# Two layer norms behind the last MLP of a four-layer transformer: later turns, the first applied by ScalarE

## The chip, the cores and the metric

The kernel runs on one core of a Trainium2 chip. The metric is the device time of one execution in microseconds, lower is better. The numbers shown are the median of several executions, and one execution that the hardware profiler recorded. The engines are called PE (TensorE, matrix products), DVE (VectorE), ACT (ScalarE), POOL (GpSimd) and SP (SyncE, which issues the DMAs); PEld is TensorE's loading of weights.

## The reference

Eight blocks in a row, each added to the residual stream `x` with a norm in front and one behind. The input has 16 sequences of 256 tokens with 128 features, all float32. The part that matters here is the end of the third block and the beginning of the fourth:

```python
x = x + layernorm(L1_attn(layernorm(x)))     # block 3: a transformer of its own
x = x + layernorm(L1_ffn(layernorm(x)))      # block 4: soft mixture of 64 experts

def L1_attn(z):                              # four layers
    for i in range(4):
        z = z + attention(layer_norm(z, g1, b1)) # 4 local heads, 4 linear heads
        h = layer_norm(z, g2, b2)
        z = z + (gelu(h @ W1[i] + b1[i]) @ W2[i] + b2[i])
    return z

def L1_ffn(m):
    logits = einsum('bmd,dnp->bmnp', m, phi)
    dispatch = softmax(logits, axis=0)       # over the batch
    combine = softmax(logits over n*p)
    slots = einsum('bmd,bmnp->bnpd', m, dispatch)
    return einsum('bnpd,bmnp->bmd', einsum('bnpd,nde->bnpe', slots, W) + b, combine)
```

Two norms without gain or bias stand between the inner transformer's last MLP and the mixture of experts: the norm of the inner result `z`, which is added to `x`, and the norm of the new `x`, which is the mixture's input `m`. A norm is (v − mean) / sqrt(var + 1e-5) over the 128 features of a token.

## The kernel before

The tokens are cut into eight groups of 512 (two sequences each). A group's data is a tile of 128 partitions by 4 token tiles by 128 features, and stays in SBUF: `x[g]` is the outer residual stream, `z[g]` the inner transformer's. The stage is `stage_l1_attn`. It makes two generators for each of 4 layers x 8 groups: `l1_mix` (attention) and `ffn` (the MLP and, in the last layer, what follows it). Each generator yields between its steps. `k.turns` goes through turns; in each turn every generator that has started is moved on by one step (up to three where it is behind its place), the latest one first. Groups start 8 turns apart, and a group's `ffn` starts 17 turns after the group's nominal start. The engines then run their instructions in the order in which they were so written (`tc.manual_schedule`); `idle(n)` is n turns in which a generator writes nothing. So a number of idle turns decides behind which instructions of the other groups a step stands in every engine's queue.

The names that matter for the steps:

- `k.stats(v)`: four `bn_stats` (L255) and four `bn_aggr` (L257) on VectorE give mean and variance (`ln_st`, `ln_mv`), and GpSimd makes the reciprocal root `ln_rs` in two instructions on 128x4 elements, a multiply-add (L244) and a power (L245).
- `k.stats_nb(v)`: the same, and two more GpSimd instructions on 128x4 (L274, L275) for `ln_nb`, minus mean times root.
- `k.normed`: applies a norm with four VectorE instructions of 128x128 (L264). `k.normed_act` applies it with four ScalarE activations of 128x128, scale `ln_rs` and bias `ln_nb` (L283).
- `k.residual(x, y, wait)`: stats of y, `wait` turns, `k.normed` into `ln_y`, and a GpSimd add of 128x512 into x (L303).
- `then(g, wait)` is `fill` of `soft_inputs`: a DMA copies `x[g]` to DRAM (`xs`, 256 KB, SP's queue), then `stats_nb(x[g])`, `wait` idle turns, and `normed_act` into `mxn[g]`, the mixture's input.
- `l1_ffn`: norm of z into `xn` (stats, a turn, L264 on VectorE), three turns, four transposes on TensorE (L325), ScalarE's `xT` (L811), GpSimd's add of the bias row to z (L818, 128x512), the two products with `mlp_h` on ScalarE between (L824), and VectorE's `z` from `ps_o` (L834).
- `l1_mix`: norm and transposes likewise; GpSimd's add of a bias row (L848); `qT`, `kT`; in two halves VectorE's `qm` and `q` (L874, L875) and ScalarE's `kr`, `ke`, `l_val`, `l_lin` (L876 to L879); in two batches the `b_negmask` products and scores on TensorE and VectorE's maxima `l_max` (L899, four of 128x384) with a 128x4 minimum behind (L900); transposes of the maxima (L913); VectorE's `l_ctx` (L936) and GpSimd's (L937); in two batches the exponentials `e` on ScalarE (L949) and two causal masks on GpSimd (L952); products into `ps_o`, ScalarE's `oT` (L969), VectorE's `cat` (L982, L993), ScalarE's `catT` (L999), and VectorE's `z` (L1002).

In this stage PSUM's eight banks are a ring of seven for all tiles but the outputs, and one bank, `ps_o`, which the attention's and the MLP's outputs share. Groups 6 and 7 (`k.over`) take no part in the edited lines: their norms are done inside the next stage.

In the last layer the eight groups pass one after another, one every 22 to 25 us. While a group's MLP and norms run, the next group's MLP and the attention of the ones after it fill the engines; behind group 5's norms no attention is left.

The functions that the diff touches, as in the kernel before:

Of the kernel before, what the change touches and what calls it, by code (L numbers as in the profile page):

```python
# [25 lines left out]
ALU = mybir.AluOpType  # L26
# [3 lines left out]
NB, SEQ, P, D = 16, 256, 128, 128  # L30
NG, NT, GT = 8, 4, 512
# [154 lines left out]
def idle(n):  # L186

    for _ in range(n):
        yield


def bc(ap, axis, n):

    ap = ap.unsqueeze(axis)
    shape = list(ap.shape)
    shape[axis] = n
    return ap.to_broadcast(shape)
# [554 lines left out]
def rest_of_l0(k, x, z, y):  # L752

    yield from k.residual(x, y, 3)
    yield
    nb, rs = k.stats_nb(x)
    yield from idle(3)
    k.normed_act(z, x, nb, rs)


def stage_l1_attn(k, x, ws, rows, z, then, xn, y7, xT0):


    nc = k.nc

    k.l1_val = [k.t([P, NT, 4, 32], f"l1_val{i}", 1) for i in range(3)]
    k.l1_lin = [k.t([P, NT, 65], f"l1_lin{i}", 1) for i in range(3)]
    k.l1_ctx = [k.t([P, 4, 68], f"l1_ctx{i}", 1) for i in range(2)]  # L770
    k.l1_max = [k.t([P, 2, 3, 4, 32], f"l1_max{i}", 1) for i in range(2)]
    for a in k.l1_val + k.l1_lin:
        nc.vector.memset(a, 1.0)
    for a in k.l1_max + k.l1_ctx:
        nc.gpsimd.memset(a, 0.0)
    for a in k.l1_ctx:
        nc.gpsimd.tensor_copy(a[:, :, 64:68], bc(k.c["head16"], 1, 4))
    k.cb = {n: k.t([P, P], "b_" + n, 1, dt=BF16) for n in ("ident", "negmask")}
    for n, a in k.cb.items():
        nc.vector.tensor_copy(a, k.c[n])  # L780

    def ffn(i, g):
        late = i == 3 and g in k.over
        yield from l1_ffn(k, z[g], ws[i], rows[f"b2{i}"], xn[g] if late else z[g])
        if i == 3 and not late:
            yield from idle(2)
            yield from k.residual(x[g], z[g], 2)
            yield
            yield from then(g, 2)

    at = [0, 5, 11, 16, 22] + [32 + 8 * n for n in range(4 * NG - 5)]
    items = []
    for n, start in enumerate(at):
        i, g = divmod(n, NG)
        items.append((start - (0 if n == 0 else 4), l1_mix(k, z[g], ws[i], rows[f"bo{i}"], n, xT0 if n == 0 else None)))
        items.append((start + 17, ffn(i, g)))
    items = sorted(items, key=lambda item: -item[0])
    with k.tc.manual_schedule():  # L800
        k.turns(items + [(0, rest_of_l0(k, x[NG - 1], z[NG - 1], y7))])
# [13 lines left out]
def l1_ffn(k, z, w, b2, out):  # L815

    hT = yield from l1_norm_T(k, z, w["ln2_g"], w["ln2_b"], 1, 3)
    k.nc.gpsimd.tensor_tensor(z, z, bc(b2, 1, NT), ALU.add)  # L818
    yield
    h = k.t([P, 4, GT], "mlp_h", 2)  # L820
    for f in range(4):
        ps = k.ps("s")
        k.mm(ps, w["w1"][:, f * P : (f + 1) * P], hT)
        k.nc.scalar.activation(h[:, f, :], ps, AF.Gelu, bias=w["b1"][:, f : f + 1])  # L824
        if f % 2:
            yield
    ps = k.ps("o").rearrange("p (t d) -> p t d", t=NT)
    w2 = w["w2"].rearrange("p (c n) -> p c n", c=4)
    for t in range(NT):
        for f in range(4):  # L830
            k.mm(ps[:, t, :], h[:, f, t * P : (t + 1) * P], w2[:, f, :], f == 0, f == 3)
        if t in (0, 2):
            yield
    k.nc.vector.tensor_tensor(out, ps, z, ALU.add)  # L834
# [1252 lines left out]
```

## Time and profile before

| quantity | value |
|---|---|
| time, median of 3 executions | 2942.89 us (2938.27 to 2943.25) |
| profiled execution, its own time | 2940.6 us |
| its span | 2938.8 us |
| granted TensorE clock, mean over the span | 0.973 |
| TensorE busy | 2729.7 us, 93% |
| VectorE busy | 1953.3 us, 66% |
| ScalarE busy | 1717.5 us, 58% |
| GpSimd busy | 1017.2 us, 35% |
| instructions | 59589 |
| edited part within the span | about 787 to 930 us |

The span is the time from the first to the last recorded instruction of the profiled execution; what lies around it makes 1.8 us. Busy times are sums over the engine's instructions. In the lines of the profile, a row of a timeline begins with the start and the duration in microseconds, then engine, source line, operation, output and inputs with their shapes, how many instructions were joined (x4), and in brackets the idle time of the engine ahead of it and what ended that. In the table of windows each row has the stretch, its length, the busy time of the engines with the number of instructions, the granted TensorE clock, the DMA share and GB/s.

### The profile page before, as it was taken

How to read it: one execution, taken by the hardware profiler on the slowest of the kernel's cores; microseconds unless marked ns; L12 is line 12 of the kernel's file. 1: busy time of each engine (PE TensorE's matmuls, PEld its weight loads, DVE VectorE, ACT ScalarE, POOL GpSimd, SP SyncE). 2: the span in 40 equal slices, each digit the busy share in tenths (PEclk: the TensorE clock that was granted, in tenths of full speed). 3: DMA queues.
4: the chain of work that ended last, by engine and by line, in shares of the span. 5: the costliest groups of instructions: out<-in, count | busy, mean ns of one | idle time of the engine just before them, and what ended most of it. 6: DMA issues, size and time to landing. Idle time of an engine off the chain costs nothing.

```text
span 2938.8 us, 59589 instructions
## 1 busy us (share of the span) xinstructions
PE 2729.7 (93%) x23673; PEld 1845.0 (63%) x23674; DVE 1953.3 (66%) x5309; ACT 1717.5 (58%) x3568; POOL 1017.2 (35%) x1406
## 2 busy tenths in 40 slices
PE   8889999999998799999978998899999799989998
PEld 4556667766666588888853443566666444436897
DVE  5665666666675989999866765666574677736542
ACT  6756566666665567777735665444444277756443
POOL 3543333333345100000044555422231466545332
PEclk9999999999999899999988999899999899999999
DMA  4000000000000000000020000000000000010000
GB/s 117 12 1 1 2 1 2 2 2 2 5 12 24 1 16 9 8 9 8 9 71 5 1 1 1 1 1 1 1 1 1 2 1 1 1 33 27 2 16 16
DMA packets 29150, 31.30 MB, mean 11 GB/s; under 512 B 7292, under 2 KB 20156, under 8 KB 28732
## 3 DMA queue, kind: packets, MB, share of 16 engines
q1 hardware_dynamic: 28872, 27.49, 3.1%
q8 instruction: 187, 3.06, 0.4%
q14 instruction: 91, 0.75, 0.1%
HBM read 23.29 MB, written 4.19 MB: 9 GB/s over the span
## 4 chain that ended last, share of the span: by engine, by line
PE 69%; ACT 12%; DVE 11%; POOL 5%; issue 2%; DMA 0%; POOLq 0%; SPq 0%; ACTq 0%; DVEq 0%
PE ps_s L336 44%; PE ps_o L336 10%; PE ps_mm L336 6%; PE ps_s L325 3%; ACT e L949 2%; ACT at_e L491 1%; POOL ln_rs L245 1%; ACT lg L1215 1%; DVE xn L264 1%; PE ps_xin L336 1%; ACT meT L1222 1%; POOL e L952 1%; PE ps_sum L336 1%; ACT L949 1%; ACT mdisp L1122 1%
## 5 line engine op out<-in xcount | busy, mean ns | idle before, releaser
L459 DVE TENSOR_REDUCE at_nm<-ps_s 128x2 f32<-128x512 f32 (+1 forms) x384 | 238.1, 682 | 119.6 <-PE ps_s L336 119.6
L491 ACT ACTIVATE at_e<-ps_s 128x512 f32<-128x512 f32 x384 | 198.2, 604 | 97.0 <-PE ps_s L336 94.8
L1504 DVE TENSOR_TENSOR scan<-ps_s,lm 128x384 f32<-128x384 f32 x256 | 124.7, 549 | 142.4 <-PE ps_s L336 142.1
L497 POOL TENSOR_SCALAR_AFFINE_SELECT at_e<-at_e 128x1024 f32<-128x1024 f32 (+1 forms) x96 | 135.1, 1407 | 209.0 <-ACT at_e L491 208.7
L245 POOL TENSOR_TENSOR ln_rs<-ln_rs,mhalf 128x4 f32<-128x4 f32 x192 | 196.1, 1021 | 15.8
L1031 POOL TENSOR_TENSOR ln_rs<-ln_mv,mendt 128x4 f32<-128x4 f32 x6 | 1.2, 200 | 521.0 <-DVE ln_mv L1029 521.0
L244 POOL TENSOR_SCALAR ln_rs<-ln_mv 128x4 f32<-128x4 f32 x184 | 39.6, 215 | 371.2 <-DVE ln_mv L257 352.8
L336 PE MATMUL ps_o<-my,meT 128*128 128x129 f32 x1024 | 142.5, 286 | 22.2 <-ACT mgot L1234 18.4
L336 PE MATMUL ps_s<-l1f_phi,mxT 128*128 128x256 f32 x512 | 141.6, 401 | 21.6 <-DVE mpart L1096 15.9
L899 DVE TENSOR_REDUCE l_max<-ps_s 128x3 f32<-128x384 f32 x256 | 124.8, 551 | 51.4 <-PE ps_s L336 49.1
L952 POOL TENSOR_SCALAR_AFFINE_SELECT e<-e 128x512 f32<-128x512 f32 x128 | 78.9, 637 | 217.2 <-ACT e L949 217.2
L336 PEld LDWEIGHTS ps_o<-my,meT 128*128 128x128 f32 x1024 | 126.3, 193 | 40.5 <-ACT mgot L1234 24.1
L336 PE MATMUL ps_s<-qm,kT 32*128 32x512 f32 x768 | 144.0, 652 | 8.0 <-DVE at_nm L459 7.8
L336 PE MATMUL ps_s<-km,qT 32*128 32x512 f32 x768 | 138.2, 667 | 11.3 <-DVE qT L1648 3.7
L336 PEld LDWEIGHTS ps_o<-l_w,mlp_h 128*128 128x128 f32 x1024 | 126.0, 192 | 19.1 <-issue 12.8
L336 PE MATMUL ps_o<-at_e,at_vm 128*32 128x128 f32 (+1 forms) x2048 | 123.2, 338 | 15.3 <-ACT at_oT L521 15.3
L336 PE MATMUL ps_o<-l_w,mlp_h 128*128 128x128 f32 x1024 | 130.1, 276 | 4.0 <-ACT oT L969 3.9
L336 PE MATMUL ps_s<-b_negmask,b_ident 128*128 128x256 bf16 (+1 forms) x640 | 123.6, 303 | 8.1 <-DVE b_negmask L780 1.4
L1481 ACT COPY BT<-ps_s 128x512 f32<-128x512 f32 x64 | 37.5, 587 | 158.1 <-PE ps_s L336 158.1
L336 PE MATMUL ps_mm<-mdisp,mxn 128*128 128x128 f32 x1024 | 125.3, 279 | 5.0 <-DVE mdisp L1134 4.9
L336 PEld LDWEIGHTS ps_mm<-mdisp,mxn 128*128 128x128 f32 x1024 | 121.8, 195 | 7.9 <-DVE mdisp L1134 6.6
L336 PE MATMUL ps_s<-xT,l_w 128*128 128x512 f32 x256 | 124.4, 607 | 1.3 <-ACT xT L811 1.3
(469 smaller groups left out, 7192.5 us busy)
## 6 DMA issues: line engine op xcount, KB each, us to landing
mw<-in_l1fw SPq DMA_DIRECT2D x16, 256.0 KB, 2.6
moe_w<-in_moe SPq DMA_DIRECT2D x16, 256.0 KB, 5.3
l_w<-in_l SPq DMA_DIRECT2D x10, 256.0 KB, 3.3
x<-in_x SPq DMA_DIRECT2D x8, 256.0 KB, 5.1
xs<-x SPq DMA_DIRECT2D x8, 256.0 KB, 2.1
out<-x SPq DMA_DIRECT2D x8, 256.0 KB, 2.3
slT<-xs SPq DMA_DIRECT2D x6, 256.0 KB, 2.8
l1f_phi<-in_l1f SPq DMA_DIRECT2D x1, 1024.0 KB, 5.0
```

The costliest lines, as they stand in the source:

```text
L244: g.tensor_scalar(out, in_, scale, eps, ALU.mult, ALU.add)
L245: g.tensor_tensor(out, out, self.mhalf[:, :n], ALU.pow)
L325: self.nc.tensor.transpose(out[:n, k * P : (k + 1) * P], src[:, k, cols], self.c["ident"])
L336: self.nc.tensor.matmul(out, lhsT=lhsT, rhs=rhs, start=start, stop=stop, skip_group_check=True)
L459: v_.tensor_reduce(nm[:, t, r, vs], s, AX.X, ALU.max, negate=True)
L491: nc.scalar.activation(e[:, r], s, AF.Exp)
L497: nc.gpsimd.affine_select(at, at, [[0, 4], [0, n], [1, P]], ALU.is_ge, 0.0, base=0, channel_multiplier=-1)
L899: v.tensor_reduce(mx[:, b, :, h, 16], s, AX.X, ALU.max, negate=True)
L949: nc.scalar.activation(e[:, h].rearrange("p j n -> p (j n)"), s[:, : 3 * P], AF.Exp)
L952: nc.gpsimd.affine_select(e[:, :, j, :], e[:, :, j, :], [[0, 4], [1, P]], ALU.is_ge, 0.0, base=0, channel_multiplier=-1)
L1481: nc.scalar.copy(s, ps)
L1504: v.tensor_tensor(m, s[:, : SEQ + P], lm[:, SCAN_HEADS[4 * (t // 2) + 2 * i + hh], :], ALU.mult)
```

## The change

In the last layer, for groups 0 to 5, `ffn` waits six turns instead of two behind the MLP before it takes the statistics of z; it takes them with `stats_nb`, so GpSimd also makes `ln_nb`; three turns later ScalarE, not VectorE, applies the norm (`normed_act` into `ln_y`); GpSimd adds it to x as before; after three turns, not one, `then` copies x to DRAM and takes its statistics, and after three more turns, not two, ScalarE writes `mxn`.

```diff
--- before.py
+++ after.py
@@ -783,10 +783,14 @@
         late = i == 3 and g in k.over
         yield from l1_ffn(k, z[g], ws[i], rows[f"b2{i}"], xn[g] if late else z[g])
         if i == 3 and not late:
-            yield from idle(2)
-            yield from k.residual(x[g], z[g], 2)
-            yield
-            yield from then(g, 2)
+            yield from idle(6)
+            nb, rs = k.stats_nb(z[g])
+            yield from idle(3)
+            y = k.t([P, NT, D], "ln_y", 2)
+            k.normed_act(y, z[g], nb, rs)
+            nc.gpsimd.tensor_tensor(x[g], x[g], y, ALU.add)
+            yield from idle(3)
+            yield from then(g, 3)
```

The written order of TensorE's and of SP's instructions is the same in both kernels. VectorE has 24 instructions fewer, ScalarE 24 more and GpSimd 12 more. Lines of the new code behind the edit stand four lines lower than those of the kernel before; the GpSimd add of x is L791 in the changed kernel.

## The prediction

> **What bounds the kernel now.** I read the page first: busy shares, then the chain of work that ended last.
>
> ```profile
> PE 2729.7 (93%) x23673; PEld 1845.0 (63%) x23674; DVE 1953.3 (66%) x5309; ACT 1717.5 (58%) x3568; POOL 1017.2 (35%) x1406
> PE 69%; ACT 12%; DVE 11%; POOL 5%; issue 2%; DMA 0%; POOLq 0%; SPq 0%; ACTq 0%; DVEq 0%
> ```
>
> TensorE bounds the whole; another engine's work costs only where TensorE waits for it. The change touches one place: the last layer's groups in the four-layer transformer, about 787 to 930 us. So next I cut the table of windows at each group period (from one group's `ps_o` block to the next), two periods without the edited norms ahead of it.
>
> ```profile
> core 0: us, PE busy (x) PEld busy (x) DVE busy (x) ACT busy (x) POOL busy (x), PEclk, DMA share, GB/s
> 765.08:787.57 22.49, 22.25 (x220) 15.70 (x219) 14.22 (x51) 14.28 (x30) 7.84 (x12) 1.00 0.00 1
> 787.57:812.15 24.58, 23.34 (x219) 15.71 (x218) 18.25 (x71) 15.62 (x34) 11.91 (x19) 1.00 0.04 12
> 812.15:836.76 24.61, 23.36 (x220) 15.72 (x218) 18.39 (x72) 16.33 (x35) 12.30 (x19) 1.00 0.04 12
> 836.76:860.79 24.03, 23.03 (x219) 15.72 (x218) 18.24 (x72) 16.06 (x34) 11.90 (x18) 1.00 0.04 13
> 860.79:884.82 24.03, 23.03 (x219) 15.71 (x218) 18.24 (x72) 16.06 (x34) 11.89 (x18) 1.00 0.04 12
> ```
>
> An undisturbed period, U, takes 22.49 us with TensorE never idle for long. The four periods with norms, P0 to P3, take 2.09, 2.12, 1.54 and 1.54 more: 7.3 us in all, the most the edit can win there. P4 and P5 are the tail, where no new group's attention fills TensorE. Then I read two neighbours on VectorE and GpSimd (start, duration), U above, P0 below:
>
> ```profile
> 771.96 0.17 DVE L900 TENSOR_TENSOR l_max<-l_max 128x4 f32<-128x4 f32 x1
> 775.29 0.53 DVE L900 TENSOR_TENSOR l_max<-l_max 128x4 f32<-128x4 f32 x1
> ...
> 798.39 1.26 POOL L818 TENSOR_TENSOR z<-z,l1rows 128x512 f32<-128x512 f32 x1
> 798.59 1.09 DVE L900 TENSOR_TENSOR l_max<-l_max 128x4 f32<-128x4 f32 x1
> 801.40 1.11 DVE L264 TENSOR_SCALAR ln_y<-z,ln_mv,ln_rs 128x128 f32<-128x128 f32 x4
> 802.59 1.27 POOL L303 TENSOR_TENSOR x<-x,ln_y 128x512 f32<-128x512 f32 x1 [2.93 <-DVE ln_y L264]
> 803.05 1.66 DVE L264 TENSOR_SCALAR xn<-z,ln_mv,ln_rs 128x128 f32<-128x128 f32 x4
> ```
>
> A 128x4 minimum takes 0.17 us alone and up to 1.09 beside a 128x512 GpSimd add; four xn scalings take 1.66 beside L303 and 1.11 elsewhere. The old placement costs twice per period: the z statistics (0.87+0.36, about 1.06 with overlap) stand ahead of the second l_max block, and TensorE's transposes L913 wait 0.80; then ln_y and the slowed xn hold the next transposes, 0.72 more.
>
> Last, what can stretch the start of a period. ScalarE's `kr` waits for VectorE's q, which stands behind xn, which waits for the MLP's reciprocal root on GpSimd (L244, L245):
>
> ```profile
> 786.65 0.19 POOL L244 TENSOR_SCALAR ln_rs<-ln_mv 128x4 f32<-128x4 f32 x1
> 786.92 1.02 POOL L245 TENSOR_TENSOR ln_rs<-ln_rs,mhalf 128x4 f32<-128x4 f32 x1
> 787.98 1.11 DVE L264 TENSOR_SCALAR xn<-z,ln_mv,ln_rs 128x128 f32<-128x128 f32 x4 [2.71 <-POOL ln_rs L245]
> ...
> 767.22 0.28 ACT L876 ACTIVATE kr<-ps_s 128x128 f32<-128x128 f32 x1 [3.38 <-DVE q L875]
> 767.89 1.20 PE L336 MATMUL ps_s<-b_negmask,b_ident 128*128 128x256 bf16 x4
> ...
> 839.58 0.65 PE L336 MATMUL ps_s<-b_negmask,b_ident 128*128 128x256 bf16 x4
> ```
>
> The four negmask products need banks that ScalarE empties. They take 1.20 us where xn starts 0.41 us after the period's start (U), and 0.65 where it starts 0.14 ahead of it (P2: xn at 836.62). So in U and P0 this path already sets TensorE's pace, and GpSimd lateness there is paid one for one; P2 and P3 have about 0.55 us in hand.
>
> **The change part by part**, per group 0 to 5. TensorE's and SP's written order stays; VectorE's, ScalarE's and GpSimd's move.
>
> (a) Removed from VectorE: four ln_y scalings, 1.03 to 1.11 us, and the GpSimd add that slowed xn behind them. Moved: z's statistics go from between the two l_max blocks to behind `l_ctx` (L936), where VectorE sits idle 3.25 us ahead of L1002 in U. Hidden there. Gain: P0's 2.09 in full, so P0 = 22.49; the others keep U as their base too.
>
> (b) z's root now issues L244, L245 and two nb operations (0.19+1.02+0.23+0.20, starts apart: 1.74 us with the gaps) on GpSimd, behind the two e masks (L952) and ahead of the MLP's root. This queue position is what the change costs: behind it stand the MLP's L244/L245, for which xn, q, kr and TensorE's negmask products wait. In P1 nothing is in hand: +1.74. In P2 and P3 the table load ahead of e no longer waits for TensorE (e starts 4.86 us ahead of the period at 831.90, against 3.94 at 808.21): 1.74−0.92, +0.83.
>
> (c) ScalarE gets ln_y, four activations. Nearest row: mxn, the same 128x128 form, 1.64 to 1.67 us. They stand behind the second kr/ke/val/lin set and ahead of oT; ScalarE's busy share is 16 of 24 us and it idles 1.31 ahead of oT (771.52) in U. oT would be about 0.3 late, and its reader on TensorE comes over 5 us later. Taken: 0; from below 0, from above 0.3.
>
> (d) The x add (L791, 1.27 us, as L303) now comes right behind the second e mask, in my reckoning 0.27 us ahead of the first l_max block's end. The trace's rows give its price: the minimum L900 becomes 1.1 to 1.27 instead of 0.17, the second block slides, and L913 waits 0.87. Bounds: 0 (it misses L900) to 1.1. Taken: 0.87, by the row at 798.59. A rule speaks against the change here: the Trainium skill, "SBUF — State Buffer" (Who interferes with whom), says that a VectorE operation with two SBUF inputs and a GpSimd one that reads SBUF exclude each other for the whole instruction. The row's 1.09 is just the rest of L818 (ends 799.65), so it agrees; by the rule the cost is the add's full remainder, 1.27-0.27 = 1.0, by the row less the slack at L913, 0.87. I keep the row.
>
> (e) x's statistics (1.06) move a period on, just ahead of the xn that TensorE's transposes L325 wait for: 0.8 of slack there in U, so +0.25. Their root, nb and the four mxn activations move likewise; mxn is first read after 930 us, and the ScalarE gap takes them: 0 in the full periods. The fill's DMA xs<-x (256 KB, 2.0 us) goes out a period later on SP; behind it stand only later groups' copies and, at 931.4, the weight loads, which the last copy precedes by several us: 0.
>
> Sum, full periods: P1 = 22.49+1.74+0.87+0.25 = 25.35; P2 = P3 = 22.49+0.83+0.87+0.25 = 24.44. P0 to P3: 22.49+25.35+48.88 = 96.72 against 97.25. So −0.5 at the start of P4: what (a) wins, 7.3, goes back by (b) 3.4, (d) 2.6, (e) 0.75.
>
> Tail. In P4 the chain is serial: catT, e, the e masks, then GpSimd's root, xn, z (L834), and only then TensorE's `ps_o` block, which was idle 905.67 to 907.50 already. The four extra GpSimd operations (1.74) are in that chain, and P4 starts its cat transposes 0.77 late: `ps_o` at 910.0 instead of 907.50, +2.5 in all. In P5 the add of x5 follows the root at once and meets the xn scalings (TENSOR_SCALAR, as the 802.59/803.05 pair): 1.27 at most, 0.55 at least by that pair; taken 1.25, since now all of xn is behind it. Sum: +3.75, taken as +3.8, and nothing later gives it back.
>
> Against the profiled execution, 2940.6 us (span 2938.8): 2944.4. The median of the runs shown is 2942.89, 2.3 above it: 2946.7, say 2946.5.
>
> **A second rule, on the clock.** The longer wait in P4 leaves TensorE idle about 906.45 to 910.0, 3.55 us. In this trace a gap of 1.83 us (905.67) kept the clock at 1.00; a gap of 3.39 us goes with a granted clock of 0.65 in it and 0.50 in the 4.5 us behind:
>
> ```profile
> 940.10:943.50 3.40, 0.01 (x2) 0.00 (x1) 3.40 (x20) 0.37 (x1) 2.68 (x7) 0.65 0.39 139
> 943.50:948.00 4.50, 4.50 (x13) 3.68 (x14) 1.30 (x3) 3.98 (x10) 4.34 (x5) 0.50 0.00 0
> ```
>
> The skill's "TensorE: Matmul & The Clock Gate" (Part 1) halves the clock after an idle window of about 3.4 us, on a free-running window. By the row a 3.55 us gap costs half clock for 4.5 us or somewhat more, half of which is lost (+2.3 to +3.4); by the rule alone it takes a whole aligned window, so mostly not. I take 0 and keep +3 for the range.
>
> **The rivals.** *A, likeliest, 0.55:* as summed, own range 2942 to 2950. *B, 0.18:* the adds miss L900 and xn, as L245 does (slT 0.34 at 936.15 beneath a root). Then (d) and the tail's 1.25 go: 3.8−2.6−1.25 = 0, 2943. For it: a shift of 0.3 us decides. Against: the rows of both pairs. *C, 0.13, faster:* GpSimd's insert doesn't reach kr, because the e masks come a microsecond earlier than I think, as they do in P2; with 0.55 in hand and B as well the full periods fall to about 22.6, −7 there and the tail at 0: 2936. It decides from 1.2 us of slack beyond those 0.55. *D, 0.14, slower:* one mechanism, the clock drop behind the P4 gap, in the `ps_o` block and the MLP products behind it: +3 on A, 2946.7+3 = 2949.7. It decides from a gap of about 3.4 us that meets the clock's window.
>
> **How the numbers follow.** Two tenths of a per cent, 5.9 us, is about what a measurement of this kernel can tell from no change. Faster by more: most of C, 0.10, and a stray 0.02. Slower by more: D 0.14 and the upper part of A, 0.16. Between: 0.58. The range takes in B's lower end and D: 2938 to 2953.
>
> **What would show it.** Right: P0 near 22.5, P1 longest near 25.3, P2 and P3 near 24.4; negmask back at 1.2 or more in P1 to P3 with "kr <- q" the longest wait; L900 near 1.1 beneath L791; a gap over 3 us ahead of P4's `ps_o`. Wrong in (b): negmask at 0.65 in P2 and P3, periods near 22.6. Wrong in (d): first L900 at 0.17. Wrong in the tail: `ps_o` at or before 907.5 less what P0 to P3 gained. D: PEclk under 1 between 908 and 916.

## The result, and the profile after

| | changed kernel | kernel before, same chip |
|---|---|---|
| median, first comparison | 2954.99 us (2949.64 to 2957.99, 6 runs) | 2942.43 us |
| ratio to before | 1.0043, 95% interval 1.0032 to 1.0054 | |
| median, second comparison (`after_again`) | 2953.03 us (10 runs) | 2945.75 us |
| ratio to before | 1.0026, interval 1.0017 to 1.0035 | |
| profiled execution | 2957.99 us, span 2956.2 us, clock 0.966 | 2940.6 us, span 2938.8 us, clock 0.973 |

The changed kernel is slower, by 7 to 13 us. The forecast was 2946.5 us with a range to 2953; the first median lies above that range and the second on its edge. Of the 17.4 us between the two spans, 12.3 have arisen by the mixture's first transposes (931.39 before, 943.71 after). The rest arises in unchanged code: the last 540 us of the span take 5.4 more, at a mean clock of 0.96 instead of 0.97. Why the clock differs there was not followed. The profiled execution is the slowest of its six. In the second profile (`after_again`) the way from P0's start to the mixture's first transposes is 153.12 us, against 156.48 in the first and 143.82 in the kernel before: 9.3 and 12.7 us longer. (The 12.7 are the 12.3 above and 0.3 by which P0 starts earlier.) The two differ in how long the clock was halved.

The table of windows of the changed kernel, by group period P0 to P3 as before, then four stretches of the tail. The columns are stretch, length, busy time of TensorE, its weight loads, VectorE, ScalarE and GpSimd, then the granted clock, DMA share and GB/s:

```profile
787.23:809.72 22.49, 22.25 (x220) 15.70 (x219) 15.27 (x59) 14.29 (x30) 7.84 (x12) 1.00 0.01 2
809.72:835.47 25.75, 23.74 (x219) 16.45 (x218) 15.90 (x67) 17.38 (x38) 13.15 (x23) 0.93 0.03 12
835.47:860.13 24.66, 22.99 (x220) 15.65 (x219) 17.20 (x67) 17.37 (x38) 12.34 (x21) 1.00 0.04 12
860.13:884.73 24.60, 22.98 (x219) 15.65 (x218) 17.19 (x67) 17.37 (x38) 12.34 (x20) 1.00 0.03 12
...
907.00:912.33 5.33, 0.00 (x0) 0.03 (x1) 3.39 (x5) 3.15 (x8) 4.62 (x8) 0.87 0.00 0
912.33:917.00 4.67, 4.50 (x52) 2.80 (x52) 0.12 (x1) 1.36 (x2) 0.60 (x1) 0.50 0.15 56
917.00:921.00 4.00, 3.96 (x6) 1.79 (x7) 0.78 (x4) 2.12 (x3) 0.00 (x0) 0.50 0.00 0
932.20:939.00 6.80, 6.73 (x11) 2.96 (x12) 0.47 (x5) 2.12 (x5) 1.77 (x5) 0.56 0.00 0
```

P0 to P3 sum to 97.50 us, against 97.25 before: the four full periods cost nothing and won nothing, close to the forecast 96.72. The loss is in the tail, and the granted clock, the last column but two, names half of it: TensorE idle for 5.33 us, then over 8 us at half clock (a granted clock of 0.50), and half clock again from 931.4.

What holds the start of a period, in P2 (TensorE, then GpSimd and VectorE):

```profile
839.47 1.05 PE L336 MATMUL ps_s<-b_negmask,b_ident 128*128 128x256 bf16 x3 [0.91 <-ACT l_lin L883]
...
843.21 1.27 POOL L791 TENSOR_TENSOR x<-x,ln_y 128x512 f32<-128x512 f32 x1 [0.95 <-ACT ln_y L283]
843.38 1.12 DVE L904 TENSOR_TENSOR l_max<-l_max 128x4 f32<-128x4 f32 x1
```

The negmask products wait for ScalarE, and the minimum (L904 here, L900 before) takes 1.12 us beneath the x add instead of 0.17. What makes P4's gap, from GpSimd's queue to VectorE's xn to TensorE:

```profile
905.56 0.19 POOL L244 TENSOR_SCALAR ln_rs<-ln_mv 128x4 f32<-128x4 f32 x1
905.83 1.04 POOL L245 TENSOR_TENSOR ln_rs<-ln_rs,mhalf 128x4 f32<-128x4 f32 x1
...
907.44 0.19 POOL L244 TENSOR_SCALAR ln_rs<-ln_mv 128x4 f32<-128x4 f32 x1
907.72 1.04 POOL L245 TENSOR_TENSOR ln_rs<-ln_rs,mhalf 128x4 f32<-128x4 f32 x1
908.73 1.23 POOL L956 TENSOR_SCALAR_AFFINE_SELECT e<-e 128x512 f32<-128x512 f32 x2
908.79 2.79 DVE L264 TENSOR_SCALAR xn<-z,ln_mv,ln_rs 128x128 f32<-128x128 f32 x4 [3.49 <-POOL ln_rs L245]
910.24 1.26 POOL L791 TENSOR_TENSOR x<-x,ln_y 128x512 f32<-128x512 f32 x1 [0.29 <-ACT ln_y L283]
912.33 2.79 PE L336 MATMUL ps_o<-e,l_val 128*32 128x256 f32 x32 [5.39 <-DVE z L838]
```

The first root is z's (for the norm), the second the MLP's; xn waits for the second, and its four scalings then run beside the last e masks (L956) and the x add: 2.79 us instead of 1.12. The `ps_o` block behind the gap takes 2.79 us at half clock instead of 1.67. Start by start, profile against profile, the 12.3 us are: −0.1 at P4's start; +1.35 until its cat transposes (GpSimd's order at the period's start); +1.9 for z's root ahead of the MLP's; +1.7 for the slowed xn; +3.6 half clock behind the gap; +0.9 for the slowed xn of P5 (2.05 instead of 1.12 us); +2.9 half clock in the last MLP. In `after_again` the waits are the same (gaps of 5.40 and 2.01 us), but half clock cost 1.6 and 1.7 us by the same reckoning, 3.3 instead of 6.5.

### The profile page after: what moved, and what is told of

The parts are those of the page before. It is cut to its first block, busy times and chain, and to the rows that moved or that the text cites. A ratio compares the mean times of both kernels' runs of the same rounds, so it can differ in the third digit from the quotient of the medians.

```text
span 2956.2 us, 59604 instructions
## 1 busy us (share of the span) xinstructions
PE 2742.3 (93%) x23674; PEld 1852.9 (63%) x23674; DVE 1946.1 (66%) x5285; ACT 1725.7 (58%) x3592; POOL 1020.4 (35%) x1418
## 4 chain that ended last, share of the span: by engine, by line
PE 69%; ACT 13%; DVE 11%; POOL 5%; issue 2%; DMA 0%; POOLq 0%; ACTq 0%; DVEq 0%
PE ps_s L336 44%; PE ps_o L336 10%; PE ps_mm L336 6%; PE ps_s L325 3%; ACT e L953 2%; POOL ln_rs L245 2%; ACT at_e L491 1%; DVE xn L264 1%; ACT lg L1219 1%; ACT L953 1%; PE ps_xin L336 1%; POOL e L956 1%; ACT meT L1226 1%; PE ps_sum L336 1%; ACT mdisp L1126 1%
## 5 line engine op out<-in xcount | busy, mean ns | idle before, releaser
L956 POOL TENSOR_SCALAR_AFFINE_SELECT e<-e 128x512 f32<-128x512 f32 x128 | 78.9, 637 | 224.9 <-ACT e L953 224.9
L336 PEld LDWEIGHTS <-b_ident 128*128 128x128 bf16 x656 | 57.2, 99 | 114.7 <-issue 95.8
```

The costliest lines, as they stand in the source:

```text
L336: self.nc.tensor.matmul(out, lhsT=lhsT, rhs=rhs, start=start, stop=stop, skip_group_check=True)
L956: nc.gpsimd.affine_select(e[:, :, j, :], e[:, :, j, :], [[0, 4], [1, P]], ALU.is_ge, 0.0, base=0, channel_multiplier=-1)
```

## The experiments

Three theories were held against each other. Q: GpSimd's queue position and the collisions of its adds and masks with VectorE set off the loss. S: ScalarE's extra activations and the later statistics of x cost. C: the clock falls in this region by itself. All ratios are to the kernel before on the same chip; most experiments were not timed beside the changed kernel, so their gain over it is told by these ratios.

**z_later.** z's statistics one turn later, so z's root stands behind the MLP's on GpSimd; the orders of TensorE, ScalarE and SP are the same. (VectorE's order changes too, but its xn waits for the root in both kernels.)

```diff
-            yield from idle(6)
+            yield from idle(7)
             nb, rs = k.stats_nb(z[g])
-            yield from idle(3)
+            yield from idle(2)
```

> The statistics of z one turn later (idle 7, then 2), so that GpSimd makes the MLP's root ahead of z's root and nb; everything else of the change stays. Theory Q (GpSimd's queue position sets off the loss): the negmask wait goes, P1 falls from 25.75 to about 22.5-23.5 and P2, P3 from 24.6 to about 23.5; in P4 xn starts 1.9 us earlier, ahead of the last e mask and the x add, so the gap ahead of ps_o falls from 5.39 to about 2 us and the clock stays up; all in all 12 to 16 us less than the changed kernel, about 2940. Rival S (ScalarE's extra activations and the later x statistics are what costs): no gain from this order alone, 2953 to 2957. Rival C (the clock drops by itself in this region): at most the 5 us of the waits come back, about 2949.

Measured: 2943.05 us, ratio 1.0005 (0.9997 to 1.0013). The place of z's root on GpSimd carries nearly all of the loss. In P4 (VectorE, TensorE) and at the last MLP (ScalarE, TensorE):

```profile
899.88 1.11 DVE L264 TENSOR_SCALAR xn<-z,ln_mv,ln_rs 128x128 f32<-128x128 f32 x4 [0.57 <-POOL ln_rs L245]
901.73 1.67 PE L336 MATMUL ps_o<-e,l_val 128*32 128x256 f32 x32 [1.83 <-POOL ln_nb L275]
...
916.61 1.65 ACT L283 ACTIVATE ln_y<-z,ln_nb,ln_rs 128x128 f32<-128x128 f32 x4 [3.95 <-POOL ln_nb L275]
918.98 5.89 PE L336 MATMUL ps_s<-xT,l_w 128*128 128x512 f32 x8 [2.72 <-ACT xT L815]
```

xn follows the root at once, takes 1.11 us, and the gap is 1.83 as in the kernel before. (Its row names `ln_nb` as the releaser, which these products do not read; z from `ps_o`, L838, ended at 901.59.) By the ratios the run gained 6 to 11 us, where 12 to 16 were expected, for a reason that the expectation missed: group 5's ln_y now stands late in front of the last xT on ScalarE, a new gap of 2.72 us and half clock behind it (5.89 us instead of 3.70). P1 to P3 were 23.66, 23.06 and 23.07 us, with a wait of 0.50 at L917 in each: the first minimum took 1.12 us beneath the x add, the second 0.80 beneath the MLP's bias add.

**add_later2.** Only the six x adds move, behind the MLP's bias add on GpSimd and so behind xn.

```diff
             k.normed_act(y, z[g], nb, rs)
+            yield from idle(2)
             nc.gpsimd.tensor_tensor(x[g], x[g], y, ALU.add)
-            yield from idle(3)
+            yield from idle(1)
```

> Only GpSimd's six adds of ln_y to x come two turns later, behind the bias add of the MLP (and so behind xn). Theory Q with the port collision: xn takes 1.9 instead of 2.79 us in P4 and 1.1 instead of 2.05 in P5; the gaps fall to about 4.2 and 1.1 us, the clock drop behind P5 goes, the one behind P4 stays; L904 of the second block may collide instead (+0.5 per period): about 2951. Rival S: the adds are not what costs, 2954 to 2956.

Measured: 2947.17 us, ratio 1.0019 (1.0011 to 1.0028), a larger gain than expected. P4's gap is 4.35 us:

```profile
911.10 1.75 DVE L264 TENSOR_SCALAR xn<-z,ln_mv,ln_rs 128x128 f32<-128x128 f32 x4 [3.49 <-POOL ln_rs L245]
```

xn with only the e masks beside it takes 1.75 us: of the 1.67 that it lost in P4, about 0.65 are the masks' and 1.0 the add's. The feared collision of the second minimum did not grow: it took 0.52 to 0.54 us, as in an undisturbed period, and P2 and P3 fell from 24.6 to 23.66, a whole microsecond each. One part of the expectation failed: P5's gap fell to 1.07 us, but half clock still came behind it, at 932.60.

**keep_warm** and **keep_warm2.** The changed kernel with products on TensorE that nobody reads, in the idle time of the tail.

```diff
+    if n == 4 * NG - 1:
+        ps = k.ps("mm")
+        for _ in range(9):              # 5 in keep_warm2
+            k.mm(ps, k.c["ident"], kT)
     o = k.ps("o")
...
+    if warm is not None:                # the last MLP only
+        ps = k.ps("mm")
+        for _ in range(3):              # 2 in keep_warm2
+            k.mm(ps, k.c["ident"], warm)
     ps = k.transposed_ps(xn)
...
+    if warm:                            # not in keep_warm2
+        ps = k.ps("mm")
+        k.mm(ps, k.c["ident"], w["w1"])
```

> The changed kernel with 13 products on TensorE whose result nobody reads: nine of 128x512 in the gap ahead of P4's ps_o, three ahead of the last xn transposes, one ahead of the last MLP's first product. They fill idle time and take no wait away. If the gaps pull the clock down (theory Q's second half): granted clock 1.00 from 907 to 940 and 6.5 us less, about 2948.5. If the clock drops by itself or for the sum of work (rival C): still half clock there, 2955. If the products lie in the way: slower.

Measured: 2950.44 us, ratio 1.0032 (1.002 to 1.0045). The clock stayed at 1.00 from 907 to 936, but nine products took 7.99 us where 5.39 were idle: about 2.3 of the 6.5 us went back.

> As keep_warm, with five and two unread products and none ahead of the last MLP: a 128x512 product took 0.89 us there, not the 0.49 reckoned with, so they fit the gaps of 5.39 and 2.01 us this time. If the gaps pull the clock down: 6 us less than the changed kernel (4.9 in the first, 1.0 to 2.9 in the second), 2948 to 2949. If the clock drops for another reason: 2954 to 2955.

Measured: 2949.82 us, ratio 1.0023 (1.0013 to 1.0033). All waits of the changed kernel are still there, only their idle time is filled. The windows from `ps_o` on (the stretch 928.60 to 932.00 is the beginning of the last MLP, 932.20 in the changed kernel's table):

```profile
912.43:917.00 4.57, 4.10 (x56) 2.56 (x57) 0.91 (x4) 2.92 (x4) 0.61 (x1) 1.00 0.17 61
917.00:921.00 4.00, 4.00 (x23) 2.67 (x22) 2.78 (x18) 2.88 (x5) 1.20 (x3) 1.00 0.00 0
928.60:932.00 3.40, 3.40 (x8) 1.62 (x9) 0.41 (x5) 1.89 (x3) 1.71 (x5) 1.00 0.00 0
```

Full clock in the three places that had 0.50, 0.50 and 0.56. The way from P0's start to the mixture's first transposes is 149.54 us, 6.9 and 3.6 less than in the changed kernel's two profiles. The medians show less: the interval overlaps that of the changed kernel's second comparison (1.0017 to 1.0035). C falls by the profiles: with the idle time filled, the tail kept its clock in both keep_warm profiles, and the changed kernel's two profiles lost it twice each.

**tail_old.** The old lines for groups 4 and 5, the new ones for 0 to 3.

```diff
+            if g < 4:
...
+            else:
+                yield from idle(2)
+                yield from k.residual(x[g], z[g], 2)
+                yield
+                yield from then(g, 2)
```

> Groups 4 and 5 keep the old code, groups 0 to 3 the new. Theory Q: nearly all of the loss is in the tail (P4, P5 and the clock behind them), so it comes back but for P4's late start (about 1.3 us): 2943 to 2945. Rival S (the cost lies in each group's norms): two of six groups' share comes back, about 2951.

Measured: 2950.75 us, ratio 1.0029 (1.0018 to 1.0041). This is S's number and not Q's, but the trace shows another cause:

```profile
913.70 2.79 PE L336 MATMUL ps_o<-e,l_val 128*32 128x256 f32 x32 [2.56 <-DVE z L844]
```

Group 3's root and its x add fall into P4, and make it 2.5 us later at the cat transposes (the expectation had 1.3: it forgot the collision at L904); the gap becomes 2.56 us, and that is enough for half clock behind it, and again in the last MLP: 3.0 us. Up to the mixture this run takes 150.08 us, 6.3 more than the kernel before, where the changed kernel's profiles take 12.7 and 9.3 more. So groups 4 and 5 carry a third to a half of the loss, not nearly all of it. Against S itself speaks the next run.

**act_only** and **dve_norm** take the two parts of the change one by one: the old turns with ScalarE, and the new turns with VectorE.

```diff
             yield from idle(2)                     # act_only
-            yield from k.residual(x[g], z[g], 2)
+            nb, rs = k.stats_nb(z[g])
+            yield from idle(2)
+            y = k.t([P, NT, D], "ln_y", 2)
+            k.normed_act(y, z[g], nb, rs)
+            nc.gpsimd.tensor_tensor(x[g], x[g], y, ALU.add)
             yield
             yield from then(g, 2)
...
-            nb, rs = k.stats_nb(z[g])              # dve_norm, from the changed kernel
+            mv, rs = k.stats(z[g])
-            k.normed_act(y, z[g], nb, rs)
+            k.normed(y, z[g], mv, rs)
```

> The turns of the kernel before, with ScalarE applying the first norm (24 activations, 12 more GpSimd operations). Theory Q (turns and queue position cost, not the engine): z's statistics stay ahead of the second l_max block (0.8 at L913 stays), xn is no longer behind ln_y (0.7 gained), mlp_h comes up to 0.7 later behind ln_y on ScalarE: 2939 to 2943, as the kernel before. Rival S (ScalarE's extra work costs): 2947 or more.

Measured: 2939.67 us, ratio 0.9990 (0.9983 to 0.9996): a little faster than the kernel before. S falls: ScalarE's 24 activations cost nothing that shows. P1 takes 22.84 us, P0 to P3 together 91.17, 6.1 less than before; half clock in the last MLP took 1.7 of that back in the profile. The wait at the second l_max block is nearly gone, though z's statistics still stand ahead of it:

```profile
844.74 0.17 DVE L904 TENSOR_TENSOR l_max<-l_max 128x4 f32<-128x4 f32 x1
845.01 1.28 POOL L822 TENSOR_TENSOR z<-z,l1rows 128x512 f32<-128x512 f32 x1
```

The two nb operations push the MLP's bias add (L822) on GpSimd back by 0.4 us, so the minimum is through before it starts, and takes 0.17 instead of 1.09 us.

> The turns of the change, with VectorE applying the first norm (no nb operations). Theory Q: z's root still stands ahead of the MLP's root, 1.3 instead of 1.74 us; gaps in P1 to P4 about 0.45 shorter; in P4 the add falls behind xn since ln_y does, so xn meets only the e mask: gap ahead of ps_o 3.7 us, clock still down behind it: 2948 to 2951. Rival S: the loss goes with ScalarE's part, 2941 to 2943.

Measured: 2946.76 us, ratio 1.0016 (1.0009 to 1.0024), lower than expected and well above act_only. P4's gap is 3.85 us; P1 and P2 are 25.38 and 25.40. So the turns lose without ScalarE's part. At these turns that part adds something in P4 through GpSimd, where the gap is 5.39 us: two nb operations more, and an x add early enough to meet xn.

**best** joins what the others point to.

```diff
-            yield from idle(6)
+            yield from idle(7 if g < 5 else 6)
             nb, rs = k.stats_nb(z[g])
-            yield from idle(3)
+            yield from idle(2 if g < 5 else 3)
             y = k.t([P, NT, D], "ln_y", 2)
             k.normed_act(y, z[g], nb, rs)
+            yield from idle(2)
             nc.gpsimd.tensor_tensor(x[g], x[g], y, ALU.add)
-            yield from idle(3)
+            yield
             yield from then(g, 3)
```

> z's statistics one turn later for groups 0 to 4 (behind the MLP's root on GpSimd), at the change's turn for group 5, and all six adds two turns later. If the queue position and the port collisions are the whole of the loss, the two gains add up: P1 to P3 at 22.1 to 22.7 us (z_later's 23.1 to 23.7 less about 1.0 of collisions), the gap ahead of P4's ps_o 1.83, ahead of the last xn transposes 1.07, and no 2.72 us gap ahead of the last MLP: 7 us less than the kernel before, 2933 to 2937. If they overlap or a new wait takes their place: 2940 to 2943.

Measured: 2936.65 us, ratio 0.9984 (0.9976 to 0.9992); a second time (`best_2`) 2936.47 us, ratio 0.9978 (0.9969 to 0.9986). It is 5 to 6 us faster than the kernel before, and by the ratios 12 to 19 us faster than the changed kernel. Its windows P1 to P3 (of best_2; P0 took 22.50 us):

```profile
810.32:833.04 22.72, 22.48 (x220) 15.70 (x218) 16.74 (x69) 17.39 (x38) 13.05 (x23) 1.00 0.04 13
833.04:855.16 22.12, 22.12 (x220) 15.73 (x218) 16.29 (x68) 17.59 (x38) 12.29 (x21) 1.00 0.04 14
855.16:877.27 22.11, 22.11 (x219) 15.73 (x218) 16.28 (x68) 17.58 (x38) 12.30 (x21) 1.00 0.04 13
```

TensorE is busy in every microsecond of P2 and P3, with both norms beside it: 89.45 us for four periods, 7.8 less than before.

**best_warm** puts two unread products into best's 1.84 us gap and one into the 1.08 us gap.

> The version best with two unread 128x512 products in the 1.84 us gap ahead of P4's ps_o and one in the 1.08 us gap ahead of the last xn transposes. If gaps of this size pull the clock down in most executions: no half clock from 899 to 926 and 2 to 3 us less than best, 2933 to 2935. If they do so only by chance of one execution: as best, 2936 to 2937.

Measured: 2935.40 us, ratio 0.9961 (0.9948 to 0.9975), on a chip where the kernel before took 2945.75. Beside best on one chip (`best_2`, `best_warm_2`):

> The version best again, beside best_warm on one chip: 5 to 6 us less than the kernel before.

> best_warm again, beside best on one chip. If gaps of 1.84 and 1.08 us pull the clock down in most executions: 2 to 3 us less than best. If seldom: within 1 us of it.

best_2 2936.47, best_warm_2 2934.44 us, ratio 0.9964 (0.995 to 0.9977). The two intervals overlap: a gain of 2 us over best is not shown. Both profiles with the products have full clock up to the mixture; best and best_2 do not.

**after_again**, the changed kernel on the chip of best_warm, which took 17.6 us less there.

> The changed kernel again, on the same chip as the above: 2953 to 2956. If the clock spells behind the 5.39 and 2.01 us gaps are no accident of the one profile, they are here too; the one behind the 1.77 us gap in P1 may or may not be.

Measured as in the first table: gaps of 5.40 and 2.01 us and half clock behind both, as in the first profile, but for a shorter time (6.83 and 3.41 us instead of 10.24 and 6.83). P1 took 25.57 us, without the half clock that the first profile had there.

## Why the prediction was wrong

**The full periods: right in sum, and in most of the mechanism.** (a) P0 was 22.49 us as forecast. (b) The negmask wait came back; P1's start slipped by 1.99 us (forecast 1.74), P2's by 1.03 (0.83); the four GpSimd operations take 1.87 us from the first root's start to the next, where 1.74 was taken. (d) and (e) In P2 the wait at L917 cost 0.96 (0.87), and x's statistics 0.18 (0.25); P2 is 24.66 against 24.44. In P1 the profile shows 25.75 against 25.35 with other parts: half clock for some 3 us cost 1.4, and the minimum then missed the add (0.30 us). (c) ScalarE's own time at 0 holds, by act_only.

**The reading of before: one wait had the wrong cause.** The prediction put the 0.80 at L913 down to z's statistics. act_only keeps the statistics where they were and loses most of the wait, since the minimum no longer meets the bias add. So the statistics were nearly covered, and the collision was the cost.

**The tail: a term left at nothing.** The prediction had P4's `ps_o` block 2.5 us late. Measured: 4.8 (912.33 against 907.50). The late start of the cat transposes came at 1.3 where 0.77 was taken, and z's root at 1.9 where 1.74 was taken. The slowed xn, 1.67 us, was not in the sum at all. The rule on the port had been applied to L904 and to P5's xn, but in P4 the forecast had xn at its old length, although the masks and the x add stand right behind the root in the same queue. P5's own collision was +0.9 where 1.25 was taken. Without the clock the tail lost 5.8 us where 3.75 was summed.

**The clock: the step that failed most, taken at 0.** It cost 6.5 us in one profile and 3.3 in the other. Rival D, given 0.14, happened, and twice in each. The prediction reasoned that only a whole aligned window of idle time halves the clock, so that a gap of 3.55 us would mostly escape. The gap became 5.39 us, and the window need not be idle as a whole. The clock records of the 14 profiles show it. In each, every spell of half clock begins on one grid with a step of 3.413 us, within 1 ns over the whole program, and lasts a whole number of steps (but for the last one recorded). Divide the stretch from 787 to 931 us of each along its grid, and take the windows at full clock. Where TensorE was idle for 1.9 us or more of a window, half clock followed in 12 of 12; below 1.4 us in none of 156; between in 5 of 12. Over the whole programs it is 245 of 247, 53 of 3747 and 47 of 205, so the edge is narrow but not exact. Two equal gaps, in best_2 and in the kernel before:

```profile
896.93:900.35 3.42, 1.59 (x33) 1.22 (x32) 2.08 (x10) 2.27 (x6) 3.17 (x7) 1.00 0.00 0
900.35:903.76 3.41, 3.33 (x47) 1.96 (x36) 0.03 (x1) 2.31 (x5) 3.04 (x3) 0.50 0.00 0
...
903.60:907.01 3.41, 2.07 (x27) 1.74 (x26) 1.81 (x10) 2.08 (x7) 1.84 (x4) 1.00 0.01 2
907.01:910.43 3.42, 2.65 (x52) 1.56 (x52) 1.71 (x10) 1.52 (x3) 2.80 (x5) 1.00 0.00 0
```

In best_2 the gap of 1.83 us lies within one window, and the next one has half clock. In the kernel before the grid cuts the same gap into 1.34 and 0.49 us, and the clock stays. (In z_later such a gap lies within one window and the clock stays too; why is open.) The Trainium skill, "TensorE: Matmul & The Clock Gate" (Part 1), has the clock halve after an idle window of about 3.4 us, on a free-running window. The free-running window is in these profiles; that all of it must be idle is not, and the measurement decides. By the measured step, a gap of 3.55 us has at least 1.77 us in one window wherever it falls, and 1.9 or more in about nine positions of ten (an estimate). So half clock was likely even at the forecast gap. The full clock in this stretch of the kernel before was luck of the grid's position: behind gaps as long as its own, half clock came in two of five profiles ahead of P4's `ps_o` and in five of seven ahead of the last MLP (gaps of 1.07 and 0.87 us).

**The median against the profile** added 2.3 us to the forecast, and was harmless: the medians of before were 2941 to 2946 over the comparisons.

## What to carry to other kernels

When a step moves to another engine or turn, write down every queue that it now stands in and what is right behind it: here four tiny GpSimd operations, 1.9 us, stood ahead of the MLP's reciprocal root, and one turn of difference returned 6 to 11 us. Check each long GpSimd operation against every SBUF-to-SBUF VectorE operation that can fall beside it, in the tail as well as in the steady part. Where TensorE waits, ask how much idle time can fall into one 3.41 us window of the clock, short gaps added up. In these profiles half clock came behind every gap of 2 us or more in this stretch, so count it as part of the wait's price; where the wait is shorter, widen the range by it.

## What the runs showed of the hardware

- Four 128x128 tensor_scalar (1.11 us alone) took 1.75 to 1.77 us beside two 128x512 affine_selects and 2.79 beside the selects and a 128x512 add. The 128x4 power on GpSimd, 1.01 us long, did not slow them: four took 1.11 us beside it (z_later, 899.88).
- The last MLP's first four products, 128x128 by 128x512 in float32, took 3.70 us at full clock and 6.65 almost wholly at half. An unread product of this size took 0.89 us. The profile records each as two instructions (x8 for these four, x18 for keep_warm's nine).
- Unread products in TensorE's idle time kept the clock at 1.00 in the tail up to the mixture; with five and two products the way there took 3.6 and 6.9 us less than in the changed kernel's two profiles. By the medians the gain was not clear of noise, nor was it where the gaps were 1.84 and 1.08 us.
- Half clock set in and ended only on a grid of 3.413 us, the same through a whole program and at other positions in other executions; a window with 1.9 us or more of TensorE idle was followed by half clock in 245 of 247 cases.
